# Building a token table from one-hot rows laid out in pairs, with the shared expert's work placed after the table

## Chip, cores, metric

One core of a Trainium2 chip. The metric is the device time of one execution in microseconds (us); the kernel before took 893.26 us in the median of three runs (889.21 to 894.62).

## What is computed

`x` holds 16 x 128 tokens of 512 numbers. First a cross attention is added (32 query heads, 8 key heads of 16, keys and values are both `ctx_512`). Then a mixture of experts is added:

```
xn   = layernorm(x)
s    = sigmoid(xn @ gate.T);  tidx, tw = 8 of 32 experts, from the 4 best of 8 groups; tw = 2.5 * s / sum
g, u = xn @ w1[e].T, xn @ w3[e].T
routed = sum over chosen e of tw * ((silu(g) * u) @ w2[e].T)
shared = (silu(xn @ sw1.T) * (xn @ sw3.T)) @ sw2.T
out  = x + routed + shared
```

Everything is float32 in the reference; an expert has 256 inner features.

## The kernel before, in words

**Order of work.** Attention runs first, two half-steps per batch of 128 tokens, with the layernorm and gate logits woven in. Its last part already starts the shared expert. Then `experts` (L1044) does four things:

1. `route()` (L1124) chooses experts from the logits, on VectorE, while TensorE does *up* products of the shared expert. Each expert has a fixed run of slots (capacities in `CAPS`, sorted by size; in all 138 slices of 128 slots). Every token has eight choices; `sr` and `sq` hold, for each choice, the place in its slice (0 to 127) and the slice (0 to 137).
2. The *table* `token` (128 x 138): which token sits in which slot. For each of the 16 tiles of 128 tokens, `slot_tokens` (L1009) makes one-hot rows and multiplies them: `hr` (128 tokens x 8 choices x 128 places) compares the row of numbers `slot_r` with `sr`; ScalarE scales it by the token's number into `ht` (L1022); `hq` (8 choices x 138 slices) compares `slice_q` with `sq`, one instruction per choice, six on VectorE and two on POOL (L1023 to 1026). Eight matmuls (L1030) add `ht`-transposed times `hq` into the bank `tok`. The tiles `hr`, `hq` and `ht` come from the pool `oh` with two buffers each. `finish_tokens` (L1038) turns `tok` into `token`.
3. Slices of tokens are *gathered* from `rows` in DRAM, which holds the normalized tokens and the 32 weights of each token (`gather`, L1458, an indirect DMA issued by POOL, eight buffers `xgs`), *turned* so that features lie on partitions, and put into one of five buffers `half` (slices of `xall`, which before held `xnT`, the normalized tokens turned).
4. Each expert is two *pieces* of tokens. Expert 0 and expert 31 are computed directly (`up`, L1572). The others take seven half-size products instead of eight (`seven`, L1663), for which VectorE makes `weight_sums` (L1602) and `token_sums` (L1631). `down` (L1779) multiplies by `w2`, ScalarE scales by the weight (L1804), and POOL adds the rows into the output in DRAM by indirect DMA (L1760).

**Two ways to turn.** The first ten slices (`by_PE = last_slice(3)`, pieces 0 to 3, which is experts 0 and 1) are turned on TensorE (`turn`, L1473: per slice eight matmuls against the identity, then ScalarE copies from PSUM, L1501, in `turned`). All later slices go the other way: VectorE transposes 32 x 32 blocks into one of nine `blocks` buffers (`transpose`, L1547), and `block_copies` (L1509) yields copies, each on 32 partitions, that put the blocks in place, three of four or more on ScalarE, the rest on VectorE (L1545). `weigh` (L1551) picks the slice's weights, and frees its `xgs` buffer for the next gather (`gather_next`, L1815).

**The shared expert.** `shared_up` (L271) is a generator: each `next` issues one matmul call of 512 columns; eight of them, in two banks `gu` (pool `ps_gu`), make one half of the inner features for 512 tokens. The silu (L286, in the list `later`) and the product (L289, in `products`) are queued as functions and run at a later point of the program. There are eight such pieces; the first is done in attention, seven through `up_matmuls` (L1120): 20 + 4 + 9 calls in `route`, the other 23 behind it. `shared_down` (L1363) makes 128 tokens' output (two matmul calls, banks `ps_y` and `ps_z` in turn); `add_down` (L1375) adds it to `x` and sends it to `out` on SP's queue.

**Order around the change.** All compute engines run in the order of the program (`manual_schedule`); nothing is reordered. In the loop over the 16 tiles (L1382), two up calls follow each tile's table matmuls (L1405) until none is left, and the 16 downs are spread: one per odd tile, more in the last four tiles, seven behind `finish_tokens` and one behind the first turn (L1409 to 1420, L1835 to 1838). Evictions of an iteration's products run one or two iterations later (`meanwhile`). [...] `ps_y`, `ps_z`, two `ps_gu`, two in `ps_rt`, two in `ps_sm`; `early.close()` (L1421) frees six of them for `ps_p`. `x_only.close()` (L1839) frees the memory of `x` for the pool `late`.

In the main loop over pieces (L1860) a piece has 3, 4 or 7 steps. Two lists of side work, `on_DVE` and `on_ACT`, each entry with a cost, are dealt out in proportion to the steps done. Piece `n` issues transposes up to the last slice of piece `n + 4` and copies up to piece `n + 3`. In pieces 0 and 1 it also calls `turn_next(2)` at each step (L1915), and ScalarE's list is held back to the second half of piece 1 (L1919).

Of the kernel before, what the change touches and what calls it, by code (L numbers as in the profile page):

```python
# [46 lines left out]
def tile_xattn_moe(  # L47
# [129 lines left out]

    def iota(shape, pattern, mult, dtype, name, base=0):
        i = ints.tile(shape, I32, tag="i", name="i")
        nc.gpsimd.iota(i, pattern, base=base, channel_multiplier=mult)  # L180
        f = rc.tile(shape, dtype, name=name)
        nc.gpsimd.tensor_copy(f, i)
        return f
# [20 lines left out]
    ints = ctx.enter_context(tc.tile_pool(name="ints", bufs=2))  # L204
    slot_r = iota([P, P], [[1, P]], 0, F16, "slot_r")
    slice_q = iota([P, NS], [[1, NS]], 0, F16, "slice_q")
    expert = iota([P, E], [[1, E]], 0, F32, "expert")
# [800 lines left out]

    def slot_tokens(b, sr, sq, tile_q, tok, oh, engine, meanwhile=()):  # L1009

        n = tile_q.shape[1]
        hr = oh.tile([P, TOPK, P], F16, tag="hr", name="hr")
        hq = oh.tile([P, TOPK, n], F16, tag="hq", name="hq")
        full = [P, TOPK, P]
        nc.vector.tensor_tensor(
            hr,
            slot_r.unsqueeze(1).to_broadcast(full),
            sr[:, b, :].unsqueeze(2).to_broadcast(full),
            ALU.is_equal,
        )  # L1020
        ht = oh.tile([P, TOPK, P], F16, tag="ht", name="ht")
        nc.scalar.activation(ht, hr, AF.Copy, scale=token1[:, b : b + 1])  # L1022
        for k in range(TOPK):  # L1023
            engine(k).tensor_scalar(  # L1024
                hq[:, k, :], tile_q, sq[:, b, k : k + 1], None, ALU.is_equal
            )
        for f in meanwhile:
            f()
        for k in range(TOPK):
            nc.tensor.matmul(  # L1030
                tok,
                lhsT=ht[:, k, :],
                rhs=hq[:, k, :],
                start=(b == 0 and k == 0),
                stop=(b == NT - 1 and k == TOPK - 1),
            )
# [7 lines left out]
    def experts(ups, in_order, later, products):  # L1044
# [37 lines left out]

        ps_gu = early.enter_context(tc.tile_pool(name="ps_gu", bufs=2, space=PSUM, side="right"))
        ps_rt = early.enter_context(tc.tile_pool(name="ps_rt", bufs=1, space=PSUM))
# [39 lines left out]
        def route():  # L1124
# [205 lines left out]
            nc.vector.tensor_scalar(si, si, P - 1, None, ALU.bitwise_and)  # L1330
            sq = new([P, NT, TOPK], "sq", home="s1")
            nc.vector.tensor_copy(sq, qi)  # L1332
# [48 lines left out]
        held = []  # L1381
        for b in range(NT):  # L1382

            meanwhile = later + held
            held = list(products)
            if b > NT - NTB:
                meanwhile += held
                held.clear()
            later.clear()
            products.clear()  # L1390
            slot_tokens(
                b,
                sr,
                sq,
                slice_q,
                tok,
                oh,
                lambda k: nc.gpsimd if k % 4 == 3 else nc.vector,
                meanwhile,
            )  # L1400
            if b == 2:
                weights()
            if b == 6:
                flags()
            up_matmuls(2)  # L1405

            for _ in range(b % 2 if b < NT - NTB else (NT - b) // 2):
                shared_down(next(downs))
        finish_tokens(token, tok, oh)  # L1409
        for f in later + held:  # L1410
            f()
        *downs, last_down = downs
        for b in downs:
            for f in products:
                f()
            products.clear()
            shared_down(b)
        for f in products:
            f()
        products.clear()  # L1420
        early.close()  # L1421

        ps_p = ctx.enter_context(tc.tile_pool(name="ps_p", bufs=6, space=PSUM))
        tp = ctx.enter_context(tc.tile_pool(name="tp", bufs=2))
# [41 lines left out]

        H = P // 2  # L1470
        NX = 4

        def turn(js):  # L1473


            trs = [
                [ps_p.tile([P, 2, ND, H], F32, tag="p", name="trx") for _ in range(2)]
                for _ in range(-(-len(js) // 2))
            ]
            for s, j in enumerate(js):  # L1480
                for d in range(ND):
                    for h in range(2):
                        rows_of_half = slice(h * H, (h + 1) * H)
                        nc.tensor.matmul(
                            trs[s // 2][h][:, s % 2, d, :],
                            lhsT=xg[j][rows_of_half, ts(d, P)],
                            rhs=ident[rows_of_half, rows_of_half],
                            start=True,
                            stop=True,
                            is_transpose=True,  # L1490
                            tile_position=(h * H, 0),
                        )
            for s, j in enumerate(js):
                turned(j, [tr[:, s % 2] for tr in trs[s // 2]], nc.scalar.copy)

        def turned(j, tr, copy):
            for n, a, b, col in parts(j):
                for h in range(2):
                    a0, b0 = max(a, h * H), min(b, (h + 1) * H)
                    if a0 < b0:  # L1500
                        copy(  # L1501
                            half[n % NH][:, :, col + a0 - a : col + b0 - a],
                            tr[h][:, :, a0 - h * H : b0 - h * H],
                        )
            weigh(j)

        Q = P // 4

        def block_copies(n):  # L1509
# [3 lines left out]
            for q in range(4):  # L1513
                for j in slices_in(n):
                    if j < by_PE:
                        continue
                    a, b, col = next((a, b, c) for m, a, b, c in parts(j) if m == n)
# [15 lines left out]
            for q, r, lo, to, size, many in runs:  # L1533
                for c in range(4):
                    of = blocks[q * Q : (q + 1) * Q, r : r + many, :]
                    of = of.rearrange("p s (k c j) -> p s k c j", c=4, j=Q)
                    of = of[:, :, :, c, lo : lo + size]
                    dst = half[n % NH][c * Q : (c + 1) * Q]
                    at = max(0, min(to, HW - many * P))
                    dst = dst[:, :, at : at + many * P]  # L1540
                    dst = dst.rearrange("p k (s t) -> p s k t", t=P)
                    dst = dst[:, :, :, to - at : to - at + size]
                    on_ACT = c != q or q % 2 == 0
                    copy = nc.scalar.copy if on_ACT else nc.vector.tensor_copy
                    yield on_ACT, 1 + many, lambda dst=dst, of=of, copy=copy: copy(dst, of)  # L1545
# [274 lines left out]

        def turn_next(n):
            nonlocal n_turned
            js = range(n_turned, min(n_turned + n, by_PE))
            gather_next()
            turn(js)
            n_turned += len(js)

        def last_slice(n):
            return -(-pieces[n][2] // P)

        NB_BUF = 9
        by_PE = last_slice(3)
        blocks = tp.tile([P, NB_BUF, D], F32, name="blocks", bufs=1)

        turn_next(last_slice(0))  # L1835
        shared_down(last_down)
        for f in products:
# [20 lines left out]
        last_piece = len(pieces) - 1  # L1858
        n_copied = 4
        for n in range(len(pieces)):  # L1860
# [13 lines left out]
            if not odd and fast(k + 1):  # L1874
                on_DVE += [(4, f) for f in weight_sums(k + 1)]
            to_turn = last_slice(min(n + 4, last_piece)) if n else 0
            turning = [(5, lambda j=j: transpose(j)) for j in range(n_turned, to_turn)]
            n_turned = max(n_turned, to_turn)
            copying = []
            while n_copied <= min(n + 3, last_piece):  # L1880
                copying += block_copies(n_copied)
                n_copied += 1
            if n == 1:
                first = last_slice(4) - by_PE
                on_DVE += turning[:first]
                del turning[:first]
            on_ACT += [(c, f) for a, c, f in copying if a]
# [23 lines left out]
            for step in range(steps):  # L1911
                next(of_k)
                tick()
                done += dues[step]
                if n < 2 and n_turned < by_PE:  # L1915
                    turn_next(2)
                for i, (side, total) in enumerate(sides):
                    due = done / sum(dues)
                    if n == 1 and i:  # L1919
                        due = max(0.0, 2 * due - 1)  # L1920
                    while side and lefts[i] > total * (1 - due) + 0.01:
# [98 lines left out]
```

## Time and profile before

The profiled execution took 894.74 us; its span, from first to last instruction, is 893.0 us, with a mean granted TensorE clock of 0.993.

| what | number |
|---|---|
| TensorE (PE) busy | 869.7 us, 97% |
| ScalarE (ACT), VectorE (DVE) busy | 672.3 us, 629.4 us |
| POOL busy | 514.8 us |
| first comparison `hr` / last table matmul / `token` done | 149.9 / 204.9 / 205.6 us |
| first gather issued | 205.9 us |
| first turn on TensorE | 213.5 us |
| first matmul of expert 0 / of expert 1 | 219.9 / 239.8 us |
| last matmul of the shared expert done | 216.1 us |
| turning matmuls (L1484) | 80 |
| copies L1545 on ACT, on DVE | 1080 x 366 ns, 172 x 289 ns |

How to read it: PE, DVE, ACT, POOL and SP are engines, PEld is TensorE's weight load, which overlaps its matmuls; a q behind an engine's name is its sequencer or queue. A group names a line, an engine, an operation, what it writes and from what it reads. A fp32 matmul call of the program appears as two PE instructions. Busy PE is modelled from pipelined matmuls, so work on it is best measured from start to start.

### The profile page before, as it was taken

How to read it: one execution, taken by the hardware profiler on the slowest of the kernel's cores; microseconds unless marked ns; L12 is line 12 of the kernel's file. 1: busy time of each engine (PE TensorE's matmuls, PEld its weight loads, DVE VectorE, ACT ScalarE, POOL GpSimd, SP SyncE). 2: the span in 40 equal slices, each digit the busy share in tenths (PEclk: the TensorE clock that was granted, in tenths of full speed). 3: DMA queues.
4: the chain of work that ended last, by engine and by line, in shares of the span. 5: the costliest groups of instructions: out<-in, count | busy, mean ns of one | idle time of the engine just before them, and what ended most of it. 6: DMA issues, size and time to landing. Idle time of an engine off the chain costs nothing.

```text
span 893.0 us, 13862 instructions
## 1 busy us (share of the span) xinstructions
PE 869.7 (97%) x4095; PEld 543.5 (61%) x4095; DVE 629.4 (70%) x1654; ACT 672.3 (75%) x1534; POOL 514.8 (58%) x622
## 2 busy tenths in 40 slices
PE   9999999997989999999999999999999999999995
PEld 5344444544756575666666666666667777777763
DVE  7877778884587677777777777777777767777510
ACT  5888722331599799888888888898898999999821
POOL 3587652674545576656456656666655666654454
PEclk9999999998999999999999999999999999999998
DMA  9111113416657688878778877878778888876544
GB/s 318 41 48 48 49 48 114 145 62 213 176 124 181 138 222 194 183 167 180 176 163 199 185 179 180 187 178 188 195 175 190 203 187 173 197 184 136 89 69 58
DMA packets 59875, 137.14 MB, mean 154 GB/s; under 512 B 12168, under 2 KB 16392, under 8 KB 59792
## 3 DMA queue, kind: packets, MB, share of 16 engines
q0 software_dynamic: 32032, 69.25, 41.1%
q1 hardware_dynamic: 27680, 66.81, 22.1%
q8 instruction: 34, 0.56, 0.3%
q14 instruction: 49, 0.40, 0.2%
q10 hardware_dynamic: 80, 0.13, 0.0%
HBM read 96.71 MB, written 46.73 MB: 161 GB/s over the span
## 4 chain that ended last, share of the span: by engine, by line
PE 90%; issue 3%; ACT 2%; POOL 2%; DVE 1%; DMA 1%; another core or an unknown queue 0%; POOLq 0%; ACTq 0%; DVEq 0%
PE p L1651 41%; PE y L1788 24%; PE gu L278 6%; PE sc L483 5%; PE oT L499 3%; PE y L1366 3%; PE x L453 2%; PE gu L1580 2%; POOL out_dram L1760 2%; DMA out_dram<-yw,token 1%; ACT xall L1545 1%; PE tok L1030 1%; PE warm L349 1%; PE lgT L560 0%; PE lg L575 0%
## 5 line engine op out<-in xcount | busy, mean ns | idle before, releaser
L1545 ACT COPY xall<-blocks 32x256 f32<-32x256 f32 (+10 forms) x1080 | 395.6, 366 | 14.3
L1760 POOL DMA_INDIRECT out_dram<-yw,token x150 | 245.9, 1639 | 211.0 <-ACT yw L1804 86.1
L1788 PE MATMUL y<-wdn,sa 128*128 128x512 f32 (+2 forms) x672 | 259.1, 594 | 0.0
L1460 POOL DMA_INDIRECT xgs<-rows,token x138 | 154.3, 1118 | 74.0 <-DVE own L1557 26.2
L1651 PE MATMUL p<-xall,wup 128*128 128x270 f32 (+27 forms) x720 | 185.6, 394 | 1.6 <-ACT p L1700 1.6
L1651 PEld LDWEIGHTS p<-xall,wup 128*128 128x128 f32 x720 | 136.5, 190 | 46.3 <-issue 16.1
L1788 PEld LDWEIGHTS y<-wdn,sa 128*128 128x128 f32 (+2 forms) x672 | 100.9, 171 | 83.7 <-issue 71.5
L1804 ACT ACTIVATE yw<-y,wt 128x512 f32<-128x512 f32 x138 | 94.8, 687 | 69.6 <-PE y L1788 39.0
L1651 PE MATMUL p<-t,s 128*128 128x270 f32 (+27 forms) x480 | 125.6, 394 | 0.0
L1651 PEld LDWEIGHTS p<-t,s 128*128 128x128 f32 x480 | 91.1, 190 | 37.6 <-issue 22.4
L1661 DVE TENSOR_TENSOR z<-u,p 128x270 f32<-128x270 f32 (+27 forms) x96 | 48.9, 509 | 68.2 <-PE p L1651 62.2
L1548 DVE STREAM_TRANSPOSE blocks<-xgs 128x512 f32<-128x512 f32 x128 | 90.5, 707 | 0.2
L493 ACT ACTIVATE p<-sc 128x1024 f32<-128x1024 f32 x64 | 62.1, 1024 | 13.8 <-PE sc L483 13.8
L1651 PE MATMUL p<-t,wup 128*128 128x270 f32 (+27 forms) x240 | 63.8, 396 | 0.7 <-DVE z L1661 0.7
L1651 PE MATMUL p<-xall,s 128*128 128x270 f32 (+27 forms) x240 | 63.6, 396 | 0.5 <-DVE z L1661 0.4
L1651 PEld LDWEIGHTS p<-t,wup 128*128 128x128 f32 x240 | 44.9, 190 | 25.9 <-issue 14.3
L278 PE MATMUL gu<-xall,sup 128*128 128x512 f32 x128 | 59.0, 601 | 0.7 <-ACT ssl L286 0.7
L1661 DVE TENSOR_TENSOR u<-u,p 128x270 f32<-128x270 f32 (+27 forms) x48 | 24.4, 509 | 45.1 <-PE p L1651 35.5
L1024 POOL TENSOR_SCALAR hq<-slice_q,sq 128x138 f16<-128x138 f16 x32 | 35.2, 1113 | 36.3 <-DVE sq L1332 20.1
L1651 PEld LDWEIGHTS p<-xall,s 128*128 128x128 f32 x240 | 45.2, 190 | 16.9 <-issue 3.9
L1545 DVE COPY xall<-blocks 32x256 f32<-32x256 f32 (+11 forms) x172 | 45.4, 289 | 3.2
L483 PE MATMUL sc<-qT,kz 32*128 32x512 f32 x256 | 44.2, 639 | 0.5 <-DVE qT L474 0.2
(222 smaller groups left out, 996.1 us busy)
## 6 DMA issues: line engine op xcount, KB each, us to landing
wup<-in_w_dram SPq DMA_DIRECT2D x64, 512.0 KB
wdn<-in_w_dram SPq DMA_DIRECT2D x32, 512.0 KB
rows<-xn SPq DMA_DIRECT2D x16, 256.0 KB
out_dram<-x SPq DMA_DIRECT2D x16, 256.0 KB
x<-in_x_dram SPq DMA_DIRECT2D x15, 256.0 KB
out_dram<-yw,token POOLq DMA_INDIRECT x150
xgs<-rows,token POOLq DMA_INDIRECT x138
cTs<-in_cT_dram SPq DMA_DIRECT2D x4, 256.0 KB
```

The source lines that it names most:

```text
L278: nc.tensor.matmul(acc, lhsT=sup[:, w, d, ts(i, P)], rhs=xnT[k][:, d, :], start=(d == 0), stop=(d == ND - 1),)
L483: nc.tensor.matmul(scs[j // 2][:, j % 2], lhsT=kzs[b // 4 % 2][rows, b % 4, i, :], rhs=qT[rows], start=True, stop=True, tile_position=(j * ...
L493: nc.scalar.activation(p, sc, AF.Exp, scale=1.0 / HD**0.5)
L1024: engine(k).tensor_scalar(hq[:, k, :], tile_q, sq[:, b, k : k + 1], None, ALU.is_equal)
L1460: nc.gpsimd.indirect_dma_start(out=t, out_offset=None, in_=rows[:, :], in_offset=bass.IndirectOffsetOnAxis(ap=token[:, j : j + 1], axis=0) ...
L1545: yield on_ACT, 1 + many, lambda dst=dst, of=of, copy=copy: copy(dst, of)
L1548: nc.vector.transpose(blocks[:, j % NB_BUF, :], xgs[:, j % NG_BUF, 0:D])
L1651: nc.tensor.matmul(acc[:, i, 0:h], lhsT=w[:, i, d, :], rhs=x[:, d, :], start=(first and i == d == 0), stop=(i == outs[-1] and d == 1), ski ...
L1661: soon(lambda: nc.vector.tensor_tensor(out_, a, b, ALU.add))
L1760: ins = nc.gpsimd.indirect_dma_start(out=flat, out_offset=bass.IndirectOffsetOnAxis(ap=token2[:, k - 1 : k] if a else token[0:b, j : j + 1 ...
L1788: nc.tensor.matmul(y[c0:c1, :], lhsT=acts_of[k % NA][:, i, col : col + c1 - c0], rhs=wdn[k % NW][:, i, :], start=(i == 0), stop=(i == NI - 1),
L1804: nc.scalar.activation(yws[j], y, AF.Copy, scale=wt[:, j : j + 1])
```

## The change

Six edits, which belong together.

- `slot_r` and `slice_q` hold each number twice, side by side (`twice`). `sq` becomes fp16. `slot_tokens` makes `hr` and `hq` in the order (pair of choices, place, choice within the pair), each with one two-tensor comparison on VectorE. The table matmuls read their operands at a step of two numbers.
- In the loop over the 16 tiles there is one up call per tile for the first seven, and one down per odd tile: seven up calls and eight downs; the other 16 up calls and 8 downs come behind the table.
- Behind the table: gathers, eight up calls, evictions, transposes of slices 0 to 4 on VectorE, eight up calls, evictions, then eight rounds of a down, at most one transpose (up to slice 9), an eighth of the block copies of pieces 0 to 2, and the addition of the round's product.
- The turns on TensorE go (`turn`, `turned`, `turn_next`, `by_PE`); the first ten slices take the blocks' way as the others do. Copies of pieces 0 to 2 are shared as three on ScalarE to one on VectorE.
- The pool `ps_p` opens after the last shared product, and the pool `ps_gu` lives until then.
- In the main loop piece 0 deals out transposes and the copies of piece 3 as well; the exceptions for pieces 0 and 1 go.

```diff
-    def iota(shape, pattern, mult, dtype, name, base=0):
+    def iota(shape, pattern, mult, dtype, name, base=0, twice=False):
...
+            f = rc.tile([*shape, 2], dtype, name=name)
+            nc.gpsimd.tensor_copy(f, i.unsqueeze(2).to_broadcast([*shape, 2]))
...
-    slot_r = iota([P, P], [[1, P]], 0, F16, "slot_r")
-    slice_q = iota([P, NS], [[1, NS]], 0, F16, "slice_q")
+    slot_r = iota([P, P], [[1, P]], 0, F16, "slot_r", twice=True)
+    slice_q = iota([P, NS], [[1, NS]], 0, F16, "slice_q", twice=True)
...
+        def hot(line, of, n, name):
+            h = oh.tile([P, TOPK // 2, n, 2], F16, tag=name, name=name)
+            full = [P, TOPK // 2, n, 2]
+            nc.vector.tensor_tensor(
+                h,
+                line.unsqueeze(1).to_broadcast(full),
+                of[:, b, :].rearrange("p (k i) -> p k i", i=2).unsqueeze(2).to_broadcast(full),
+                ALU.is_equal,
+            )
+            return h
+
+        hr = hot(slot_r, sr, P, "hr")
+        hq = hot(slice_q, sq, NS, "hq")
+        ht = oh.tile([P, TOPK // 2, P, 2], F16, tag="ht", name="ht")
         nc.scalar.activation(ht, hr, AF.Copy, scale=token1[:, b : b + 1])
-        for k in range(TOPK):
-            engine(k).tensor_scalar(
-                hq[:, k, :], tile_q, sq[:, b, k : k + 1], None, ALU.is_equal
-            )
...
-                lhsT=ht[:, k, :],
-                rhs=hq[:, k, :],
+                lhsT=ht[:, k // 2, :, k % 2],
+                rhs=hq[:, k // 2, :, k % 2],
...
+        def evictions():
+            nonlocal held
+            fs = later + held
             held = list(products)
...
+        for b in range(NT):
+            slot_tokens(b, sr, sq, tok, oh, evictions())
...
-            up_matmuls(2)
-
-            for _ in range(b % 2 if b < NT - NTB else (NT - b) // 2):
+            if b < 2 * ND - 1:
+                up_matmuls(1)
+            if b % 2:
                 shared_down(next(downs))
         finish_tokens(token, tok, oh)
...
-                    on_ACT = c != q or q % 2 == 0
+                    on_ACT = c != q or (n > 2 and q % 2 == 0)
...
-        turn_next(last_slice(0))
-        shared_down(last_down)
-        for f in products:
+        gather_next()
+        up_matmuls(2 * ND)
+        for f in evictions() + evictions():
             f()
+        transpose_to(5)
+        up_matmuls(2 * ND)
+        for f in evictions() + evictions():
+            f()
+        copies = [f for n in range(3) for _, _, f in block_copies(n)]
+        n_copied = 3
+        downs = list(downs)
+        for i, b in enumerate(downs):
+            shared_down(b)
+            transpose_to(min(6 + i, last_slice(3)))
+            for f in copies[len(copies) * i // len(downs) : len(copies) * (i + 1) // len(downs)]:
+                f()
+            for f in products:
+                f()
+            products.clear()
+        shared.close()
+        ps_p = ctx.enter_context(tc.tile_pool(name="ps_p", bufs=6, space=PSUM))
         x_only.close()
...
-            to_turn = last_slice(min(n + 4, last_piece)) if n else 0
+            to_turn = last_slice(min(n + 4, last_piece))
...
-                if n < 2 and n_turned < by_PE:
-                    turn_next(2)
...
-                    if n == 1 and i:
-                        due = max(0.0, 2 * due - 1)
```

`transpose_to(j)` calls `transpose` and `gather_next` for each slice up to `j`.

More of the change, by code (lines that the diff above doesn't have):

```diff
@@ L175, in tile_xattn_moe @@
     more = const.tile([1, 1], I32, name="more")
-    def iota(shape, pattern, mult, dtype, name, base=0):
+    def iota(shape, pattern, mult, dtype, name, base=0, twice=False):
         i = ints.tile(shape, I32, tag="i", name="i")
         nc.gpsimd.iota(i, pattern, base=base, channel_multiplier=mult)
-        f = rc.tile(shape, dtype, name=name)
-        nc.gpsimd.tensor_copy(f, i)
+        if twice:
+            f = rc.tile([*shape, 2], dtype, name=name)
+            nc.gpsimd.tensor_copy(f, i.unsqueeze(2).to_broadcast([*shape, 2]))
+        else:
+            f = rc.tile(shape, dtype, name=name)
+            nc.gpsimd.tensor_copy(f, i)
         return f
@@ L1007, in rest, with slot_tokens @@
                 nc.sync.dma_start(out[b], xs[b])
[L1009 to L1019, printed above, removed]
-        )
-        ht = oh.tile([P, TOPK, P], F16, tag="ht", name="ht")
+    def slot_tokens(b, sr, sq, tok, oh, meanwhile=()):
+        def hot(line, of, n, name):
[11 more added lines that the diff above has]
+        ht = oh.tile([P, TOPK // 2, P, 2], F16, tag="ht", name="ht")
         nc.scalar.activation(ht, hr, AF.Copy, scale=token1[:, b : b + 1])
-        for k in range(TOPK):
-            engine(k).tensor_scalar(
-                hq[:, k, :], tile_q, sq[:, b, k : k + 1], None, ALU.is_equal
-            )
         for f in meanwhile:
@@ L1081, in experts @@
         ps_z = ctx.enter_context(tc.tile_pool(name="ps_z", bufs=1, space=PSUM))
-        ps_gu = early.enter_context(tc.tile_pool(name="ps_gu", bufs=2, space=PSUM, side="right"))
+        shared = ExitStack()
+        ps_gu = shared.enter_context(tc.tile_pool(name="ps_gu", bufs=2, space=PSUM, side="right"))
         ps_rt = early.enter_context(tc.tile_pool(name="ps_rt", bufs=1, space=PSUM))
@@ L1330, in route @@
             nc.vector.tensor_scalar(si, si, P - 1, None, ALU.bitwise_and)
-            sq = new([P, NT, TOPK], "sq", home="s1")
+            sq = new([P, NT, TOPK], "sq", F16, home="s1")
             nc.vector.tensor_copy(sq, qi)
@@ L1381, in experts @@
         held = []
-        for b in range(NT):
-            meanwhile = later + held
+        def evictions():
+            nonlocal held
+            fs = later + held
             held = list(products)
-            if b > NT - NTB:
-                meanwhile += held
-                held.clear()
             later.clear()
             products.clear()
[L1391 to L1400, printed above, removed]
+            return fs
+        for b in range(NT):
+            slot_tokens(b, sr, sq, tok, oh, evictions())
             if b == 2:
@@ L1404, in experts @@
                 flags()
-            up_matmuls(2)
-            for _ in range(b % 2 if b < NT - NTB else (NT - b) // 2):
+            if b < 2 * ND - 1:
+                up_matmuls(1)
+            if b % 2:
                 shared_down(next(downs))
         finish_tokens(token, tok, oh)
[L1410 to L1413, printed above, removed]
-            for f in products:
[L1415 to L1420, printed above, removed]
         early.close()
-        ps_p = ctx.enter_context(tc.tile_pool(name="ps_p", bufs=6, space=PSUM))
         tp = ctx.enter_context(tc.tile_pool(name="tp", bufs=2))
@@ L1468, in gather @@
             xg[j] = t
[L1470 to L1505, printed above, removed]
         Q = P // 4
@@ L1514, in block_copies @@
                 for j in slices_in(n):
-                    if j < by_PE:
-                        continue
                     a, b, col = next((a, b, c) for m, a, b, c in parts(j) if m == n)
@@ L1819, in gather_next @@
                 n_gathered += 1
[L1821 to L1826, printed above, removed]
         def last_slice(n):
@@ L1831, in experts, with transpose_to @@
         NB_BUF = 9
-        by_PE = last_slice(3)
         blocks = tp.tile([P, NB_BUF, D], F32, name="blocks", bufs=1)
-        turn_next(last_slice(0))
-        shared_down(last_down)
-        for f in products:
-            f()
+        def transpose_to(j):
+            nonlocal n_turned
+            while n_turned < j:
+                transpose(n_turned)
+                n_turned += 1
+                gather_next()
+        gather_next()
+        up_matmuls(2 * ND)
+        for f in evictions() + evictions():
+            f()
+        transpose_to(5)
[15 more added lines that the diff above has]
+        ps_p = ctx.enter_context(tc.tile_pool(name="ps_p", bufs=6, space=PSUM))
         x_only.close()
@@ L1858, in experts @@
         last_piece = len(pieces) - 1
-        n_copied = 4
         for n in range(len(pieces)):
@@ L1882, in experts @@
                 n_copied += 1
[L1883 to L1886, printed above, removed]
             on_ACT += [(c, f) for a, c, f in copying if a]
```

## The prediction

> **What bounds the kernel now.** I read the page first (shares of the engines), then the chain that ended last, then the busy times by stage, then the single groups of the stage that the diff touches.
>
> ```profile
> PE 869.7 (97%) x4095; PEld 543.5 (61%) x4095; DVE 629.4 (70%) x1654; ACT 672.3 (75%) x1534; POOL 514.8 (58%) x622
> ...
> PE 90%; issue 3%; ACT 2%; POOL 2%; DVE 1%; DMA 1%; another core or an unknown queue 0%; POOLq 0%; ACTq 0%; DVEq 0%
> ```
>
> The busy times by stage:
>
> ```profile
> 157.57:213.50 55.93, 54.66 (x235) 27.14 (x233) 44.50 (x126) 17.66 (x17) 36.48 (x34) 1.00 0.32 109
> 213.50:219.88 6.38, 2.63 (x21) 1.25 (x20) 1.94 (x9) 1.30 (x4) 4.00 (x5) 0.91 0.99 353
> 219.88:239.81 19.93, 19.93 (x129) 16.02 (x130) 8.42 (x31) 5.68 (x20) 10.81 (x11) 0.86 0.56 154
> 239.81:285.70 45.89, 42.99 (x141) 26.10 (x140) 35.78 (x88) 44.26 (x121) 20.66 (x17) 1.00 0.62 157
> 285.70:850.00 564.30, 564.30 (x2149) 382.15 (x2151) 414.31 (x1034) 494.85 (x1225) 338.65 (x239) 1.00 0.78 178
> ```
>
> The stage lines give the length, then the busy time (and instructions) of PE, PEld, DVE, ACT, POOL, the granted clock, the DMA share and GB/s. TensorE is the bound: from 285.7 to 850 it is never idle. So a microsecond of its time saved before 285.7 should arrive at the end, and only work or idleness of TensorE counts. Stages: 157.57 is the first table matmul, 213.5 the first turn, 219.88 the first matmul of expert 0, 239.81 the first seven-product matmul of expert 1. TensorE stands idle 1.27, 3.75 and 2.90 us in the stages up to 285.7, and its clock sinks to 0.86 in the third.
>
> The groups (name, count, then nanoseconds at least, median, at most, and first and last start):
>
> ```profile
> L1015 DVE TENSOR_TENSOR hr<-slot_r,sr x16: 1208/1215/1225, 149.9 to 201.8; 128x1024 f16<-128x1024 f16 x16
> L1024 DVE TENSOR_SCALAR hq<-slice_q,sq x96: 242/289/378, 151.1 to 203.7; 128x138 f16<-128x138 f16 x96
> L1030 PE MATMUL tok<-hq,ht x128: 221/223/233, 157.6 to 204.7; 128*128 128x138 f16 x128
> L1172 DVE TENSOR_TENSOR eq<-eq,tri x1: 692/692/692, 126.4 to 126.4; 128x1024 f16<-128x1024 f16 x1
> L1169 DVE TENSOR_TENSOR gt<-gs x1: 1226/1226/1226, 124.0 to 124.0; 128x1024 f16<-128x1024 f32 x1
> ```
>
> Two slices of the same table by stage, at the end of the table:
>
> ```profile
> 216.00:218.00 2.00, 0.13 (x1) 0.00 (x0) 0.00 (x0) 0.37 (x1) 1.37 (x2) 1.00 1.03 368
> ...
> 220.00:222.00 2.00, 2.00 (x5) 1.64 (x6) 0.00 (x1) 0.00 (x0) 0.14 (x1) 0.50 0.62 186
> ```
>
> 1024 fp16 comparisons take 1215 ns when one operand's innermost step is zero (L1015), but 1024 fp16 products take 692 ns when both operands run along memory (L1172), and 1226 ns when the inputs are f32 (L1169). In 216 to 218 every compute engine nearly stops while DMA is full (368 GB/s): eight gathers and the last stores meet there. Afterwards the clock is at 0.50.
>
> [...]
>
> **The change part by part.**
>
> *Table rows, VectorE.* Per token tile one TENSOR_TENSOR of 1024 and six TENSOR_SCALAR go; two TENSOR_TENSOR of 1024 and 1104 come. Queued operations start sooner than their durations say: L1169 and the next start 1.13 us apart, so the share that overlaps is about 0.1. In pairs: 0.692 - 0.1 = 0.59 and (1104/1024 x 0.53 + 0.06) = 0.63, sum 1.23 us. Before: 1.13 + 6 x 0.19 = 2.3. Bounds: 1.23 [...], 2.34 [...] (1.13 + 1.21), more if repeated pairs are read slowly. I take 1.23, since L1172 already broadcasts an outer dimension at full rate. POOL loses 32 operations (35 us), none on the path. ScalarE's ht stays at 1.15 us.
>
> *Table matmuls.* From start to start, eight of them plus two shared-up calls take 2.26 us (158.07 to 160.33); a call is two instructions 0.43 apart, so four take 1.72 and the table's eight 0.54, 67 ns each. With operands at step two: from 0 to +123 ns each (the f32 weight load takes 190 ns); I take 0.
>
> *TensorE's work between 157.57 and 239.81.* 23 remaining up calls x 0.86 = 19.7 (46 rows of L278 after 158), 16 shared downs x 1.71 = 27.4 (the chain's rows of L1366), 16 x 0.54 = 8.6, expert 0's 64 instructions of 256 columns x 0.216 = 13.8. Sum 69.5; the stage lasted 82.24. The other 12.7: five turns x 0.64 = 3.2 (the chain's rows of L1484), idle 1.27 + 3.75 = 5.0, low clock 3.0 (eight matmuls in 3.71 and in 2.38 for 1.73, a turn in 1.05 for 0.64), small gaps 1.5. The moved up and down calls cost TensorE the same wherever they stand.
>
> *New timeline.* ht(0) is ready 0.5 earlier, so the 0.75 us in which TensorE waits for a silu queued behind it (L286) goes: start 156.85. In the first seven tiles TensorE bounds: a pair of tiles costs 2 x 0.54 + 2 x 0.86 + 1.71 = 4.5, VectorE 2 x 1.23 + 0.6 plus a product now and then. From tile 7 there are no up calls left: TensorE 2.8 a pair, VectorE 3.1, so it waits 4.5 x 0.3, of which its lead covers a part: 1.0. The last table matmul ends near 185; token is ready at 185.5 instead of 205.6, and the first gather starts near 185.8 (before: 205.92).
>
> After it TensorE still has 16 up calls (13.7) and 8 downs (13.7). Under these run: eight gathers at 1.3 us each on POOL; in before data moved about 2.5 to 3.5 us after the first issue, so slice 0 is there at 189.3, slice 4 at 194.5. VectorE first does the product of piece (3,0), near 193.9, then five transposes with weigh at 0.76 (232.67 to 233.43), then the product of (3,1), near 200.8. In the downs' loop VectorE does per down a transpose 0.76, copies 0.6 and the addition 0.6, 1.96 against TensorE's 1.71, for five downs; then 1.2. Two banks absorb most: idle 0.5. ScalarE starts its 36 block copies near 197; at 0.40 to 0.51 they end at 212.5. Expert 0 needs them only at 214.5. Without the downs as cover these 15 us would stand on the path.
>
> Start 156.85 + 69.5 + 1.0 + 0.5 + gaps of 1.1 (the 1.5 less those around the turns) = 228.9 for expert 1's first seven-product matmul, instead of 239.81: **-10.9 us**. The low clock is avoided [...].
>
> *Behind 239.81.* ScalarE was late there: 4 + 4 of the 18 copies of piece 4 had waited for expert 0's last silus, and TensorE waited 1.65 for the copy L1700, then for VectorE. Now piece 4's copies are spread over the whole of piece 1. Demand on ScalarE during expert 0 is 21 + 18 copies x 0.4 plus four silus = 17.2 against 13.8, but it starts ahead by 2 us. The silu's tile lies where x was, so it may wait for the last store (VectorE waited 2.00 for such a store in before). Its lag at expert 1 is then 1.5 to 5 us, against 7.8 before. Bounds: all 2.9 saved, or nothing. I take 2.4 saved.
>
> *The rest.* POOL's two doubled casts at the start add about 0.3 us in front of 10.5 us of idleness. SP's queue has the same loads and stores; eight stores now fall near 203 to 216, behind the gathers instead of among them. What is late next if the gathers are late: VectorE's transposes, then the second product behind them, then shared_down(12).
>
> Sum: 893.0 - 10.9 - 2.4 = 879.7 of span. The profiled execution took 894.74 for a span of 893.0, and the median of the runs is 893.26, almost the span: 880.
>
> **Rivals.**
> *A new wait after the table* (0.16): gathers and stores fill DMA again and the engines pause as at 216 to 218, or ScalarE's copies are late. For: the gathers alone bring 278 KB per 1.3 us, 214 GB/s. Against: in before ten stores shared those microseconds. A pause of 3 to 8 us: 885 (883 to 888).
> *The pairs don't pair* (0.07): 2.34 us per tile. Token ready at 149.9 + 16 x 2.34 + 10.5 (additions, products, weights, flags, finish) = 197.8, then the same 43.4 to expert 1: 241.2, and 2.4 back: 892. The change would then not do what it says.
> *Strided table operands* (0.07): +40 to +123 ns x 128 = 5 to 16 us: 884 to 895; taken as 887.
> *Slower* (0.05): reading one 4-byte pair again and again [...]. From 2.4 us a tile the gain is gone, from about 2.96 the kernel is over 1% slower; [...]. For: no row shows this pattern. [...]
>
> **Numbers.** Forecast 0.65, its own range 875 to 885; the rivals as given. 874 to 890 holds the forecast, the new waits and half of the strided case, and leaves out the other ends. About 1% (8.9 us, 884.3) is what a measurement can tell from no change. Faster by over 1%: 0.65 x 0.95 + 0.16 x 0.4 + 0.07 x 0.3 = 0.70; slower: 0.05 and the tail of the strided case, 0.06; within: 0.24.
>
> **What would show it.** Right: the two comparisons near 690 and 730 ns; token ready near 185; table matmuls at 67 ns; no idle stretch above 1 us on TensorE between 157 and 229; no clock below 0.9 there; expert 1's first product near 229; idleness after it below 1 us up to 275. Wrong: comparisons near 1200 ns, table matmuls over 100 ns apart, all engines pausing together behind the gathers, or TensorE waiting for ScalarE at expert 0 or 1.

## The result and the profile after

The changed kernel took 885.78 us in the median of ten runs (884.21 to 888.05), the kernel before 892.74 (889.21 to 895.78): a ratio of 0.993, 95% interval 0.991 to 0.995. The forecast was 880, so about half of the expected 13 us came. The profiled execution took 885.71 us with a span of 883.9, against 894.74 and 893.0 before: 9.1 us of span less.

The page of the changed kernel, engine shares and the chain that ended last:

```profile
PE 864.2 (98%) x4015; PEld 540.4 (61%) x4015; DVE 626.0 (71%) x1599; ACT 689.6 (78%) x1570; POOL 479.3 (54%) x590
...
PE 86%; issue 3%; DVE 3%; POOL 3%; DMA 2%; ACT 1%; another core or an unknown queue 0%; SPq 0%; POOLq 0%; DVEq 0%; ACTq 0%
```

TensorE is still the bound. Its 80 turn instructions are gone, and its busy time fell by 5.5 us. VectorE is now on the chain with 3% instead of 1%; the chain below shows where.

Its busy times by stage (length, then PE, PEld, DVE, ACT, POOL, the granted clock, the DMA share, GB/s). The stages are the table, the shared expert behind it, expert 0, and the stretch from the first seven-product matmul of expert 1; then two single microseconds:

```profile
157.47:186.50 29.03, 28.23 (x173) 16.05 (x172) 25.11 (x47) 16.45 (x15) 0.00 (x0) 1.00 0.37 128
186.50:219.73 33.23, 30.39 (x67) 13.03 (x66) 18.69 (x54) 18.84 (x44) 18.29 (x18) 0.95 0.71 203
219.73:233.54 13.81, 13.81 (x65) 12.16 (x64) 11.23 (x25) 10.42 (x27) 1.99 (x2) 1.00 0.29 88
233.54:283.00 49.46, 48.86 (x162) 30.27 (x161) 38.60 (x95) 47.52 (x128) 24.36 (x19) 1.00 0.66 166
...
205.00:206.00 1.00, 0.00 (x0) 0.00 (x0) 0.00 (x0) 0.98 (x3) 0.11 (x1) 1.00 0.69 222
209.00:210.00 1.00, 1.00 (x2) 0.45 (x2) 1.00 (x3) 0.98 (x3) 0.60 (x1) 0.50 0.14 51
```

Only the second stage is out of line: TensorE stood idle for 2.84 us and had a clock of 0.95 on average. In 205 to 206 neither TensorE nor VectorE did anything; from 208.4 the clock was 0.50 for 3.4 us. Expert 0 starts at 219.73, where 214.5 was forecast.

The groups of the table (count, then ns at least, median, at most, and first and last start):

```profile
L1018 DVE TENSOR_TENSOR hr<-slot_r,sr x16: 679/683/693, 149.8 to 183.2; 128x1024 f16<-128x1024 f16 x16
L1018 DVE TENSOR_TENSOR hq<-slice_q,sq x16: 724/726/735, 150.4 to 183.8; 128x1104 f16<-128x1104 f16 x16
L1033 PE MATMUL tok<-hq,ht x128: 222/224/238, 157.5 to 185.6; 128*128 128x138 f16 x128
```

The paired comparisons run at the pace hoped for, 683 and 726 ns where 690 and 730 were forecast, and the table matmuls at step two last 224 ns where the dense ones lasted 223.

The chain of waits of the changed kernel (start, length, what):

```profile
203.14 0.28 DVE xall L1486
203.42 3.44 another core or an unknown queue
206.88 0.70 DVE x L1380
...
207.63 12.26 PE y L1370 x24
219.89 13.81 PE gu L1521 x64
```

At 203.42 VectorE had reached the addition for shared_down(8). That addition waits for TensorE alone, and TensorE's last matmul of shared_down(8) ends at 203.07 by the trace. TensorE did four instructions more, to 204.79, and then needed the bank that the addition empties. Everything hung on a signal that came late. A signal is here the rise of a semaphore, of which the trace keeps the times: an instruction of one engine raises it and one of another waits for it (the addition starts at 206.88, 0.02 us behind a rise at 206.86). TensorE's read:

```
                                last matmul ends   signal rises
changed kernel, shared_down(8)       203.07           206.86
changed kernel, shared_down(9)       204.79           206.96
kernel before, turn                  213.97           217.50
kernel before, turn                  214.21           218.88
kernel before, shared_down(15)       216.13           218.94
```

Both signals of the changed kernel rise 0.10 us apart, though four instructions of 0.43 us lie between them. By the trace the matmuls had been done and their signals had been held; since the ends of matmuls are modelled, it could also be that their last results came late, and VectorE would see the same. The pause of the kernel before, at 216 to 218, looks the same. Only TensorE is touched: in all twenty traces, up to 860 us, no recorded signal of VectorE, ScalarE or POOL rises more than 0.04 us behind the end of an instruction that raises it.

### The profile page after: what moved, and what is told of

Same layout as the page of the kernel before. It is cut to its first block, busy times and chain, and to the rows that moved or that the text cites. A ratio compares the mean times of both kernels' runs of the same rounds, so it can differ in the third digit from the quotient of the medians.

```text
span 883.9 us, 13625 instructions
## 1 busy us (share of the span) xinstructions
PE 864.2 (98%) x4015; PEld 540.4 (61%) x4015; DVE 626.0 (71%) x1599; ACT 689.6 (78%) x1570; POOL 479.3 (54%) x590
## 4 chain that ended last, share of the span: by engine, by line
PE 86%; issue 3%; DVE 3%; POOL 3%; DMA 2%; ACT 1%; another core or an unknown queue 0%; SPq 0%; POOLq 0%; DVEq 0%; ACTq 0%
PE p L1592 42%; PE y L1729 24%; PE gu L282 5%; PE sc L487 4%; PE oT L503 3%; POOL out_dram L1701 3%; PE y L1370 2%; PE x L457 2%; DMA out_dram<-yw,token 2%; PE gu L1521 2%; DMA cn<-in_c_dram 1%; DVE blocks L1489 1%; PE tok L1033 1%; PE lgT L564 0%; PE lg L579 0%
## 5 line engine op out<-in xcount | busy, mean ns | idle before, releaser
L1486 ACT COPY xall<-blocks 32x256 f32<-32x256 f32 (+10 forms) x1137 | 419.0, 369 | 15.1
L1592 PE MATMUL p<-xall,wup 128*128 128x270 f32 (+27 forms) x720 | 185.5, 394 | 0.0
L1489 DVE STREAM_TRANSPOSE blocks<-xgs 128x512 f32<-128x512 f32 x138 | 97.4, 706 | 0.2
L1486 DVE COPY xall<-blocks 32x256 f32<-32x256 f32 (+11 forms) x187 | 51.1, 297 | 3.5
L1583 DVE TENSOR_TENSOR t<-xall,t 128x540 f32<-128x540 f32 (+27 forms) x60 | 43.4, 723 | 0.5
```

The source lines that it names most:

```text
L1489: nc.vector.transpose(blocks[:, j % NB_BUF, :], xgs[:, j % NG_BUF, 0:D])
L1583: yield lambda o=out_, a=a, b=b: nc.vector.tensor_tensor(o, a, b, ALU.subtract)
L1592: nc.tensor.matmul(acc[:, i, 0:h], lhsT=w[:, i, d, :], rhs=x[:, d, :], start=(first and i == d == 0), stop=(i == outs[-1] and d == 1), ski ...
```

## The experiments

**Theory A**: the unbroken row of gathers, one each 1.3 us, holds TensorE's signals back; without it the forecast holds. **Theory B**: the pause belongs to this place in the engines' streams.

The runs came in groups, each on one chip and with the kernel before timed beside it: e1 to e4, e5 to e7, e8 to e11, e12 and e13, e14 and e15, e16 to e18; the last two groups had the same chip. Each trace is one execution, each time a median of several.

**e1 and e7: fewer gathers in flight.** The edit, shortened:

```
 def gather_next():
-    while n_gathered < NS and (n_gathered < NG_BUF or n_gathered - NG_BUF in weighed):
-        gather(n_gathered)
+    while n_gathered < NS and (n_gathered < PACE
+            or n_gathered - (PACE if n_gathered < 16 else NG_BUF) in weighed):
+        ins = gather(n_gathered).ins
+        if PACE <= n_gathered < 16:
+            tc.add_manual_dep(ins, owns[n_gathered - PACE].name, SYNC)   # PACE = 4
```

> The changed kernel with at most four gathers in flight at the start: gather j (4 to 15) waits for VectorE's weigh of slice j-4. Theory A (the long unbroken row of gathers is what holds TensorE's signals back, for 3.8 us at 203): no wait above 1 us of VectorE for TensorE between 200 and 216, no clock below 0.9 there, first matmul of expert 0 near 216 instead of 219.7, time 881 to 883. Theory B (the pause belongs to this place in TensorE's or VectorE's stream and not to the gathers): the wait of 3 to 4 us and the half clock stay, 885 to 887.

Measured: 881.87 us, no late signal, TensorE busy without a break to expert 0, at 218.15 by the trace. But the kernel before took only 884.3 beside it, not 892.7 (ratio 0.9971, 0.9962 to 0.998). So what the pause costs differs from chip to chip, and this run alone proves nothing. Its profile has 6.8 us of half clock at 118.2, ahead of all that was changed, which moves everything behind it by about 3 (first gather at 189.83, in e7 at 186.92).

**e5 to e7: the two kernels and the paced one on one chip.**

> The changed kernel itself once more, on whatever chip this call gets. The kernel before took 884.3 on the chip of the last call and 892.7 on that of the first comparison, so the pause may belong to the chip or the launch and not to the kernel. Theory P (the pause comes and goes, and the kernel without it is the forecast's): where the trace shows no late signals, expert 0 starts near 216 and the time is 880.5 to 882; where it shows them, 885 to 888. Theory Q (the pause is the changed kernel's own): 885 to 886 with the pause in the trace, whatever the kernel before does.

> The kernel before once more, on the same chip, for its trace. Theory P: without the pause at 216 to 219 and the half clock behind it, first seven-product matmul of expert 1 near 234 instead of 239.81, time 884 to 887; with it 889 to 895. Theory Q: the pause is in every trace of it.

> The changed kernel with at most four gathers in flight, beside the changed kernel on the same chip. If the row of gathers makes the pause: this one shows none even where the changed kernel does, and is 3 to 5 us faster than it there. If not: the same time as the changed kernel within 1 us, pause or no pause.

Measured: before 888.98, changed 883.91 (ratio 0.9948, 0.9928 to 0.9967), paced 882.45 (0.993, 0.9912 to 0.9948); e6, the kernel before again, 889.38. TensorE's timeline, first of e5 (start, length, what, and in brackets the idle time ahead of it):

```profile
204.05 3.60 PE L1370 MATMUL y<-sdn,sa 128*128 128x512 f32 x8
209.73 12.26 PE L1370 MATMUL y<-sdn,sa 128*128 128x512 f32 x24 [2.09 <-DVE x L1380]
```

then the same stretch of e7 in the busy times by stage:

```profile
203.00:216.00 13.00, 13.00 (x33) 5.74 (x32) 12.43 (x33) 12.63 (x30) 5.08 (x5) 1.00 0.84 251
```

e5 stood for 2.09 us and then had 3.4 us of half clock, and its signals for shared_down(8) and (9) came 3.03 and 2.10 us late; e7, with the same streams on TensorE, VectorE and ScalarE, lost nothing, at a DMA share of 0.84. That speaks for A and against B, in the trace. The medians differ by 1.5 us where 3 to 5 were expected, and their intervals overlap. Part of that is the half clock ahead of the change, which comes and goes: e5's trace has 6.8 us of it at 118 and is the slowest of its six executions. Where the mean clock was 0.996 or more, four executions of e5 took 883.3 to 884.0 and three of e7 took 881.8, so pacing saved about 2 us there. In e6 a signal was late as well: VectorE waited 4.17 us to start an addition and TensorE stood 2.21 us. Theory P holds in part: the pause isn't the same everywhere.

**e8 to e11: bytes, place, and the kernel before.** In e9 the first 16 gathers fetch half-length rows; in e10 gathers 4 to 11 all wait for slice 3's weigh; e11 puts the edit of e1 into the kernel before. The edits of e9 and e10, shortened:

```
 e9   half_rows = rows.rearrange("r (a c) -> (r a) c", a=2)
      gather for j < 16:  out=t[:, 0:(D + E) // 2], in_=half_rows[:, :]
 e10  of = owns[max(n_gathered - 8, 3)]
```

> The changed kernel again, as the one to compare the other three with on the same chip. If this chip shows late TensorE signals: an idle stretch of TensorE of 2 to 3 us behind shared_down(9) and 883.5 to 886; if not, 881 to 882.

> The changed kernel whose first 16 gathers fetch rows of 1088 bytes instead of 2176, from other places, so that half of what they fetch is left out and the output is not the reference's; as many descriptors and as much of POOL's time as before. If the bytes in flight hold TensorE's signals back: no late signal, 881 to 882. If the row of POOL's gathers as such does it: late signals and the idle stretch as in the changed kernel beside it.

> The changed kernel with gathers 4 to 11 held back until slice 3 is weighed and then let go together: the long row of gathers comes 8 us later. If the row of gathers makes the pause: late signals, if at all, at 210 to 216 and not at shared_down(8), 882 to 886. If the pause belongs to shared_down(8): late signals at 203 to 207, as in the changed kernel beside it.

> The kernel before with at most four gathers in flight at the start. If the row of gathers makes the pause there too: none of the 2 to 4 us at the turns, 2 to 6 us less than the kernel before on a chip that shows the pause, about 884 to 887. If eight early gathers are needed by the turns: the time of before or up to 4 us more.

Measured: before 892.13, e8 886.51 (ratio 0.9932, 0.991 to 0.9953), e9 885.31, e10 887.74, e11 892.05. TensorE's timeline of e9 behind shared_down(9):

```profile
206.23 11.13 PE L1370 MATMUL y<-sdn,sa 128*128 128x512 f32 x24 [1.48 <-DVE x L1380]
```

VectorE's and TensorE's timelines of e10, in that order:

```profile
220.91 0.69 DVE L1380 TENSOR_TENSOR x<-y,x 128x512 f32<-128x512 f32 x1 [3.13 <-remote]
```

```profile
221.66 3.78 PE L1370 MATMUL y<-sdn,sa 128*128 128x512 f32 x4 [3.25 <-DVE x L1380]
```

e9: with half the bytes VectorE still waited for shared_down(8) until 205.48, 2.45 us after its last matmul; in e8 it was 3.93. So bytes alone are not what decides, though the hold was shorter. In e9 1.48 us of idleness cost no half clock, and the profiled execution took 883.16, the fastest of four.

e10 is the clearest run against B. Its long row of gathers began at 201.53, where e8's begins at 186.97, and the held signal moved from shared_down(8) to shared_down(13): matmul done at 216.56, signal at 220.89, where e8's came at 207.11. The row was 14.6 us later, the signal 13.8. Its time, 887.74, lies above the 882 to 886 expected: a later pause is no cheaper.

The traces also show when a hold ends. In the traces of the changed kernel (the first, e5 and e8) and in e9 and e10 the addition for the held product starts 0.4 to 1.9 us after the last gather of the row has ended (in the changed kernel 204.11 + 1.0 and 206.88). There POOL stops because its next gather needs a buffer that VectorE frees only behind the held addition (weigh at 208.12, gather at 208.60). In e6 one held signal rises while the row's last gather still runs, so this is no rule.

e11 missed its time, which was that of before (ratio 1.0004, 0.9986 to 1.0023). The signals of the first turns were prompt (the turn done at 214.49 rises at 214.54), but the held ones only moved: POOL, once let go, ran an unbroken row from 222.95, and the turn done at 228.57 reached ScalarE's copies at 235.99, 7.4 us late. TensorE stood 2.36 us between the first turn and expert 1, and 2.86 from there to 290. Pacing the first gathers did not help where a long row followed while others waited for TensorE. How long a row must be isn't settled: the first matmul held for over 1 us ended 16.2 us behind the row's start in the changed kernel, 15.0 in e10, 8.1 in the kernel before, 4.3 in e11.

**e2: spare matmuls in the idle place**, six of 512 columns behind shared_down(9).

> The changed kernel with six spare matmuls of 512 columns (0.43 us each, into a free bank) behind shared_down(9), where TensorE stood idle for 2.84 us. It adds work that nobody reads. If the half clock at 209 to 212 comes from TensorE's idleness: no clock below 0.9 there, the idle time filled, time 1 to 2 us less than the changed kernel, 884 to 885. If the clock falls with the pause itself, or if the spare matmuls only push the later ones: 886 to 888.

Measured: 886.02, against 881.55 and 881.56 for the changed kernel on another chip where nothing is held (e14, e17). No signal was held in this run, so the spare work only pushed the rest back: 4.5 us, for 12 instructions x 0.43 us = 5.2. It says nothing on the half clock.

**e3 and e4: one part each.** e3 is the changed kernel with the old slot_tokens, three comparisons of four on VectorE and one on POOL; e4 is the kernel before with the new one.

> The changed kernel with the one-hot pairs undone (rows compared one choice at a time, a quarter of them on POOL, as before), all moved work as in the changed kernel. If the pairs give the time back by an earlier table: VectorE needs 2.9 us a tile with the additions, token done near 199 instead of 186.5, everything behind it 11 to 13 us later, 895 to 898. If the moved work alone carries the gain: 886 to 888.

> The kernel before with only the one-hot rows compared in pairs; the order of the shared expert's work and TensorE's turns as before. If TensorE bounds the table (it was busy 54.66 of 55.93 us there): at most 1.3 us are to be had, 891 to 893. If VectorE or POOL set the table's pace: 885 to 888.

Measured on the chip of e1, where before takes 884.3: e3 891.84 (ratio 1.0079, 1.0065 to 1.0093), e4 885.26 (0.9995, 0.9983 to 1.0007). Who TensorE waited for in e3's table:

```profile
PE tok L1034 <- ACT ht L1026: 4.8, 5, 1.8
PE tok L1034 <- DVE hq L1028: 4.0, 3, 2.1
```

Without pairs VectorE needs 1212 ns for hr and six times 288 for hq per tile, and with one up call a tile TensorE has too little to do meanwhile: it stands 8.8 us and twice drops to half clock for 3.4 us. Expert 0 starts at 226.94, 11.6 us later than in the changed kernel without a pause (e17, below), as expected; the time expected, 895 to 898, was counted from a changed kernel with the pause. With the pairs alone no change in time can be told, because TensorE sets the old table's pace (busy for 49.15 of 49.50 us in e4). Neither part gains alone: the pairs make the short table possible, and the moved work uses it.

**e12 to e18: gathers alone, or gathers and copies; and both kernels without the pause.** e12, e15 and e18 are one kernel:

```
-copies = [f for n in range(3) for _, _, f in block_copies(n)]
+copies = [f for n in range(3) for _, _, f in block_copies(n)][:4]
```

By the traces' counts 44 copies of 48 are left out, not 46 of 50 as expected below.

> The changed kernel with 46 of the 50 block copies in the shared expert's last downs left out, so that expert 0 reads old rows and the output is not the reference's; the gathers as in the changed kernel. If the gathers alone hold TensorE's signals back: late signals of 2 to 4 us at shared_down(8) as in the changed kernel, 885 to 887 on a chip where the kernel before takes 888 or more. If it is all instructions and landings together (the traces with late signals also lose records): no late signals or far shorter ones, 880.5 to 882.5.

> The changed kernel with at most six gathers in flight at the start instead of four. If the pause grows with the length of the unbroken row of gathers: a late signal of 0.5 to 3 us, 882 to 885. If any gap in the row does: none, 881.5 to 883, as with four.

> The changed kernel beside the next one on the same chip. Where the kernel before takes about 884 and no landing is lost from the trace: no late signal, TensorE busy from the table to expert 0, expert 0 from about 216.7, 880.8 to 882. Where the kernel before takes 888 or more: late signals at shared_down(8), 884 to 886.

> The changed kernel with 46 of the 50 block copies in the last downs left out, as in e12, where the chip showed no late signal. On a chip that shows them in the changed kernel beside it: late signals of 2 to 4 us if the gathers alone make them, none or far shorter ones if the sum of gathers and copies does. On a chip that shows none: the changed kernel's time within 0.5 us, since the copies are hidden.

> The kernel before, for its trace beside the next two. On a chip without late signals: TensorE busy through the turns, first seven-product matmul of expert 1 near 233, span 882 to 884. On a chip with them: late signals at the turns, 888 to 893.

> The changed kernel beside it. Without late signals 881 to 882 and a gain of 3 to 4 us; with them 884 to 886 and a gain of 5 to 7 us.

> The changed kernel with 46 of the 50 block copies in the last downs left out, once more. On a chip with late signals: the same 2 to 4 us at shared_down(8) if the gathers alone make them, none or far shorter ones if gathers and copies together do. On a chip without: the changed kernel's time within 0.5 us.

Measured: all seven ran where no signal is held, even in the unpaced kernels. e12 881.15, e15 881.43, e18 882.56 beside e14's 881.55 and e17's 881.56. Leaving the copies out gained nothing, so they are hidden; e18 is 1.0 us slower where 0.5 was allowed, and its trace has 6.8 us of half clock at 118.7, ahead of the change. Whether the copies have a part in the pause stays open. e13 took 884.74 (0.9994, 0.9979 to 1.0009): no held signal at the downs either, but in its profile VectorE waited 5.4 us for a store of x, and TensorE 1.97 for ScalarE in expert 1, with 3.4 us of half clock behind it. It tells nothing about the length of the row.

What these runs do give is both kernels without the pause. TensorE's timeline of e17, the changed kernel:

```profile
201.34 14.17 PE L1370 MATMUL y<-sdn,sa 128*128 128x512 f32 x32
215.34 13.98 PE L1521 MATMUL gu<-xall,wup 128*128 128x256 f32 x64
229.15 1.35 PE L1592 MATMUL p<-xall,wup 128*128 128x352 f32 x4
```

and e16, the kernel before, by stage; the last line is a slice of its turns:

```profile
213.55:219.00 5.45, 5.45 (x47) 3.83 (x47) 2.06 (x10) 1.62 (x6) 4.23 (x5) 1.00 0.99 347
219.00:233.18 14.18, 14.18 (x103) 11.73 (x102) 11.35 (x36) 9.79 (x32) 10.34 (x10) 1.00 0.73 216
233.18:279.00 45.82, 45.82 (x154) 28.97 (x153) 37.00 (x89) 43.59 (x118) 24.60 (x19) 1.00 0.71 186
...
216.00:218.00 2.00, 2.00 (x13) 1.50 (x13) 1.03 (x5) 0.00 (x0) 1.41 (x2) 1.00 1.02 361
```

e17 has its first seven-product matmul of expert 1 at 229.15 (forecast 228.9) and a span of 879.9 (forecast 879.7). e16 moves 361 GB/s in 216 to 218, much as the traced kernel before did (368), with TensorE busy all the time: a full DMA alone does not make the pause. Nor does a row of gathers alone: e17 has 15 in a row from 186.98, and no signal is late. Without the pause the kernel before reaches expert 1 at 233.18 instead of 239.81, and its span is 882.2 instead of 893.0.

The five comparisons of the two kernels, in us:

| | before | changed | ratio, 95% interval |
|---|---|---|---|
| the result | 892.74 | 885.78 | 0.993 (0.991 to 0.995) |
| e8 | 892.13 | 886.51 | 0.9932 (0.991 to 0.9953) |
| e5 | 888.98 | 883.91 | 0.9948 (0.9928 to 0.9967) |
| e14 | 885.05 | 881.55 | 0.9963 (0.995 to 0.9976) |
| e17 | 884.5 | 881.56 | 0.9971 (0.9959 to 0.9982) |

In the first three, signals are held in the changed kernel's traces, and in those of the kernel before as far as there are any (e8's group has only its paced form, e11). Against the last two, which share a chip and where none are held, the kernel before is 4 to 8 us slower and the changed one 2 to 5.

**What holds the signals.** e7 and e10 tie the hold to the gathers, but not to what it is about them: POOL's work, the number in flight, their descriptors or their landings. One more thing sets the chips apart. An indirect transfer leaves 16 landings in a complete trace, 288 of them 4608. The nine traces from the chips that hold signals keep 3709 to 3905 of these landings; the eleven others keep 4602 to 4608. The nine also lack signals of TensorE, VectorE and ScalarE (678 of 730 are left of TensorE's in the changed kernel), none of them ahead of the first gather, the first one 4 to 16 us behind it. So which recorded rise belongs to which matmul is in part inferred there; the waits of VectorE are not. e7 lacks as many records as the others and shows no late signal. Missing records and late signals on the same chips could have one cause during the gathers, and it may be that recording itself has a part: a guess of the author's that no run shows, since every run here left a span and a clock, and so none was without some recording.

## Why the prediction was right and wrong

*The step that failed* is "The low clock is avoided", with the 0.5 us of idleness that went into the sum for the downs. Measured: 2.84 us idle behind shared_down(9) and 3.4 us at a clock of 0.50, which is 1.7 us of matmuls, 4.5 in all. 228.9 + 0.6 for the late start + 4.5 in place of 0.5 = 233.5; 233.54 came, so of the 10.9 us forecast up to expert 1 there came 6.3. Add the 4.5 to e17's 881.56 and it is 886.1; 885.78 was measured. There lies nearly all of the miss. Nor did it take as much as these 2.84 us: the clock fell after 2.09 us of idleness in e5 and after 1.97 in e13.

*Behind it a reading failed.* The prediction saw all engines stop beside a full DMA and put it down to eight gathers meeting the last stores; as the stores moved away, it gave the repeat 0.16. In the changed kernel no store ran between 191.1 and 207.6, and it paused; in e16, on a chip where nothing is held, stores and gathers filled DMA, and it didn't. What all the held cases share is a row of gathers while others wait for TensorE, and the change kept that: 14 gathers without a break, from 186.84. The rival "A new wait after the table", priced at 885 (883 to 888), is what happened where the signals are held; its number was right, while the full DMA that it named as the reason was not there (share 0.69 in 205 to 206).

*And the gain was counted from a paused kernel.* Of the 13.3 us forecast, 6.75 were the pause at the turns and its low clock (3.75 + 3.0 us). The first comparison got back only 2.25 of these, the difference to the new pause's 4.5. Where neither pauses the gain is 2.9 to 3.5 us, although the changed kernel is then close to the forecast's time (881.6 and 880). Where that gain comes from can be read from e16 and e17, from the first table matmul to expert 1:

```profile
157.62:233.18 75.56, 74.29 (x383) 42.71 (x382) 57.92 (x172) 29.06 (x54) 51.03 (x47) 1.00 0.45 148
157.60:229.15 71.55, 70.74 (x303) 40.50 (x302) 54.48 (x123) 45.28 (x85) 20.32 (x20) 1.00 0.52 163
```

Of 4.0 us, 3.55 are TensorE's busy time, about that of the five turns taken off it (0.71 us each as busy time, 0.64 from start to start). The earlier table serves to make room for that; no run takes the turns off by themselves.

*Right*: the price of the pairs (683 and 726 ns), an estimate until then from L1172's 692 ns, since no row of before reads pairs; no penalty for the step of two (224 ns beside 223), of which no row of before told either; token ready at 186.5 (forecast 185.5); expert 0 in 13.81 us (13.8); from the first table matmul (157.60) to expert 1, 71.55 us in e17, where the sum was 69.5 + 1.0 + 0.5 + 1.1 = 72.1; block copies and transposes hidden behind the downs.

*Off by a little*: the first table matmul came at 157.47 and not 156.85. The 0.75 us wait for the silu stayed: ScalarE was done with ht at 151.76 and then waited for TensorE's own up call until 152.43.

*Behind expert 1*: 893.0 - 239.81 = 653.2 us before and 883.9 - 233.54 = 650.4 after, 2.8 less, forecast 2.4. But this too was a gain on the pause: e16 needs 882.2 - 233.18 = 649.0 there and e17 879.9 - 229.15 = 650.8, 1.7 more. ScalarE waited 6.02 us for a store before expert 0's silu, as the prediction allowed; TensorE did not feel it.

The range, 874 to 890, held all five medians of the changed kernel, 885.78 and 886.51 because it took in the new wait.

## What to carry to other kernels

When several engines stop together, compare the end of the work with the time at which its semaphore rose before giving the stop a cause: a late signal and a full DMA look alike in a table of busy times (the stop at 205 to 206 had a DMA share of 0.69, that of the kernel before at 216 to 218 one of 1.03). A saving that consists of a stall vanishing has to be priced twice, with the stall and without, and the baseline should be traced on more than one chip before the stall counts as the kernel's. Where one engine is the bound, a gain that lasts is work taken off that engine, here the turns. Two parts of a change that are each worth nothing, or less, may be worth something together, when one makes the room that the other uses.

## What the runs showed of the hardware

- TensorE's signals can come 2 to 5 us (once 7.4, e11) after their matmuls by the trace while its queue runs on; two of them then rose 0.10 us apart in the changed kernel. VectorE's, ScalarE's and POOL's recorded signals never came more than 0.04 us late. It was seen in three groups of runs (the result, e5 to e7, e8 to e11) and not on the three chips of the other four, with the same kernels.
- Idle stretches of 1.97 (e13), 2.09, 2.84 and 2.96 us (e5, the changed kernel, e8) were each followed by 3.4 us of half clock, 3.25 and 3.75 us (e10, the kernel before) by 6.8 us; 1.48 (e9), 1.76 and 2.15 (both e3) and 2.21 us (e6) by none. In e3 stretches of 1.55 and 1.67 us, with smaller breaks beside them, were followed by 3.4 us. Even one and the same stretch differs: behind 1.17 us at 115, with breaks of 0.3 and 0.5 us after it, five of the twenty traces have 6.8 us of half clock, four 3.4 and eleven none. So the length of a stretch alone does not tell whether the clock falls; what else decides it was not shown.
